# Routed experts in four groups of slots, each read back behind its own blocks, and a conditional tail of blocks

## The chip, the cores and the metric

The kernel runs on one core of one Trainium2 chip. The metric is the device time of one launch in microseconds (us): the median of several runs. A profiled execution is used to see where the time goes; it is slower than the unprofiled runs, and its own time is given beside theirs.

## The reference

The input is `x`, two sequences of 1024 tokens with 256 features. Two layers are applied, each of which runs its mixture-of-experts feed-forward before and after its attention part (feed-forward, attention, feed-forward, with halved feed-forward residuals). In the first layer (L0) the attention part is RWKV (time mix, then channel mix), in the second (L1) a linear attention that sums over the tokens of a sequence.

The feed-forward part, cut to what matters:

```python
def moe(x):                      # x is normalized; L0: E=8, K=2, H=176; L1: E=32, K=6, H=96
    scores = softmax(x @ gate_w) # L1: sigmoid
    topk_w, topk_i = top_k(scores, K)          # L1: weights divided by their sum
    comb = zeros(T, E); comb[t, topk_i] = topk_w
    g = silu(einsum('td,edf->tef', x, wg)) * einsum('td,edf->tef', x, wu)
    routed = einsum('tef,efd,te->td', g, wd, comb)
    shared = silu(x @ sg) * (x @ su) @ sd      # hidden width 2*H
    return routed + shared

def l1_attention(X):
    Q, K, V = split(X @ W_in.T + b_in); Q, K = rope(Q), rope(K)
    A = sum_over_tokens(K / norm(K) * V)       # one row per sequence
    return (A * Q) @ W_out.T + b_out + X
```

Each token goes to K experts only, so the routed part needs K, and not E, products per token.

## The kernel before

**Tiles.** The 2048 tokens are 16 tiles of 128 (`NT`), kept in SBUF as `x`. Four tiles (`BT`) are the unit in which normalization, transposes and router logits are made (`prep`), and eight tiles (`HT`) are a half; a half is also one sequence.

**Dispatch.** `sparse_moe` handles one feed-forward part. After two `prep`s `plan(h)` gives each pair (token, expert) of its half a slot: each expert's pairs are ranked by matmuls with a triangular matrix, each expert's region is rounded up to whole blocks of 128 slots, and the slot numbers go into `idx`. `scatter(h)` then writes the normalized rows to their slots in `xs`, a buffer in HBM, by one indirect DMA for each tile and each of its K choices (line 401, on POOL). L0 has 16 of these per half, L1 has 48. The second half fills up the open last block of each expert from the first half and then goes on in new blocks. Slots that hold no token read zeros, which `fill_slots` (line 260) writes once ahead. `owners` works out, for each block, the expert that owns it; `weights(h)` takes the routing weights of each pair into `wk`.

**Blocks.** A block is 128 slots of one expert. `blocks` is a software pipeline: `fetch` reads the block from `xs` (SP's queue, line 511), `features` transposes it (PE, line 520), `inner` makes gate and up with the expert's weights, which are chosen by a register (line 542), `turn` transposes the hidden values, and `outward` makes the down product (line 559), copies it from PSUM on DVE (`yb`, line 567) and stores it to `ys` in HBM. The number of blocks is the worst case: 39 for L0 and 127 for L1.

**Reading back.** `gather(t, k)` (line 578, on POOL) reads the result rows of a tile's k-th choices by an indirect DMA, and `add_back` (line 589, on DVE) adds them, weighted, to `x`. The first half's rows lie in the first 23 (L0) or 79 (L1) blocks at most, so its gathers may start when these are stored, beside the later blocks; the second half's gathers wait for all blocks (`first` and `NBLK` in `gather`). POOL's queue is worked in order, so scatters and gathers stand in one line.

**Shared part.** `shared(h)` makes the shared expert for eight tiles on PE, beside the scatters.

**Order of the whole.** L0's first feed-forward part; the fill of L1's slots and RWKV beside it; L0's second part with the weights of L1 loading; L1's first part; attention on the first sequence beside the last gathers, then the dispatch of its half, then attention on the second sequence and the dispatch of that half; L1's second part, whose last gathers end the kernel. Within that order the instructions of each engine are put in sequence by a scheduler when the program is built; the tile pools, with their fixed numbers of buffers by tag, add waits where a buffer is used again. In attention the normalized tiles `xl` and their transposes take buffers of the tags `xn` and `xT`, the same that hold `m2`'s normalized rows. PSUM has the tags `pa`, `pb`, `pt` and `py`, two banks each: blocks use all four, `prep` and `plan` use `pt`.

Of the kernel before, what the change touches and what calls it, by code (L numbers as in the profile page):

```python
# [39 lines left out]
def moe_blocks(m):  # L40
    return (NTOK * m["K"] + m["E"] * (P - 1)) // P
# [3 lines left out]
def macaron_kernel(ctx: ExitStack, tc: tile.TileContext, a: dict, out: bass.AP):  # L45
# [28 lines left out]
    row_i = const.tile([P, 1], I32, name="row_i")  # L74
    nc.gpsimd.iota(row_i, pattern=[[0, 1]], base=0, channel_multiplier=1)
    row = const.tile([P, 1], F32, name="row")
    nc.vector.tensor_copy(row, row_i)
# [6 lines left out]
    nc.gpsimd.memset(every, 1.0)  # L84

# [18 lines left out]
    def normalize(src, dst, n, name):  # L104

        mv = small.tile([P, n, 2], F32, tag="mv", name=f"mv_{name}")
        for i in range(n):
            st = small.tile([P, 6], F32, tag="st", name=f"st_{name}_{i}", bufs=4)
            nc.vector.bn_stats(st, src[i])
            nc.vector.bn_aggr(mv[:, i, :], st)  # L110
        rstd = small.tile([P, n], F32, tag="rstd", name=f"rstd_{name}")
        nc.scalar.activation(rstd, mv[:, :, 1], AF.Sqrt, bias=eps)
        nc.vector.reciprocal(rstd, rstd)
        for i in range(n):
            nc.vector.tensor_scalar(  # L115
                dst[i], src[i], mv[:, i, 0:1], rstd[:, i : i + 1], ALU.subtract, ALU.mult
            )
# [15 lines left out]
    def route(w, lg, name, taken=None, comb=None):  # L133
# [41 lines left out]
        else:  # L175
            tot = small.tile([P, BT], F32, tag="tot", name=f"tot_{name}")
            nc.vector.tensor_reduce(tot, comb, AX.X, ALU.add)
            nc.vector.tensor_scalar(tot, tot, 1e-20, None, ALU.add)
            nc.vector.reciprocal(tot, tot)
            nc.vector.tensor_scalar(tot, tot, 0.5, None, ALU.mult)  # L180
# [6 lines left out]
    def sparse_tiles(pool, layer):  # L187
# [17 lines left out]
            blocks=moe_blocks(m),  # L205
# [61 lines left out]
    HT = NT // 2  # L267
    WHO = 4

    def sparse_moe(layer, w, nth, xs, ys, moe, last=False):  # L270

        name = f"{layer}_{nth}"
        E, K, H, C, HP, NBLK = (w[k] for k in ("E", "K", "H", "C", "HP", "blocks"))
        SH, SU, rows = w["SH"], w["SU"], w["rows"]

        first = (HT * P * K + E * (P - 1)) // P
        xs, ys = xs[0 : NBLK * P, :], ys[0 : NBLK * P, :]
        taken = moe.tile([P, NT, E], F32, tag="taken", name=f"taken_{name}")
        comb = moe.tile([P, NT, E], F32, tag="comb", name=f"comb_{name}")
        past = moe.tile([P, NT + 1, E], F32, tag="past", name=f"past_{name}")  # L280
        slot = moe.tile([P, NT, E], F32, tag="slot", name=f"slot_{name}")
        top = back.tile([P, NT, 8], F32, tag="top", name=f"top_{name}", bufs=2)
        idx = back.tile([P, NT, K], I32, tag="idx", name=f"idx_{name}", bufs=2)
        wk = back.tile([P, NT, K], F32, tag="wk", name=f"wk_{name}", bufs=2)
        who = moe.tile([P, P], I32, tag="who", name=f"who_{name}", bufs=2)
        ends = moe.tile([P, 2, E], F32, tag="ends", name=f"ends_{name}")
        xn = [moe.tile([P, HT, D], F32, tag="xn", name=f"xn_{name}_{h}", bufs=2) for h in range(2)]
        xT = [
            moe.tile([P, DC, HT * P], F32, tag="xT", name=f"xTs_{name}_{h}", bufs=2)
            for h in range(2)  # L290
        ]
        scattered, stored, far = [], [], {}

        def prep(b):
            sub = f"{name}_{b}"
            h, o = divmod(BT * b, HT)
            ts = slice(BT * b, BT * b + BT)
            xb = [xn[h][:, o + i, :] for i in range(BT)]
            normalize(x[ts], xb, BT, sub)
            for c in range(DC):  # L300
                nc.scalar.copy(xT[h][:, c, o * P : o * P + TB], transposed(xb, c, sub))
            lg = bank("pt", f"lg_{sub}")[:, 0 : BT * E].rearrange("p (t e) -> p t e", e=E)
            for i in range(BT):
                for c in range(DC):
                    nc.tensor.matmul(  # L305
                        lg[:, i, :],
                        xT[h][:, c, (o + i) * P : (o + i + 1) * P],
                        w["router"][:, c, :],
                        start=(c == 0),
                        stop=(c == DC - 1),  # L310
                    )
            route(w, lg, sub, taken[:, ts, :], comb[:, ts, :])

        def running(src, sub):

            end, d = src, 1
            while d < E:
                nxt = small.tile([P, E], F32, tag="end", name=f"end_{sub}_{d}", bufs=3)
                nc.vector.tensor_copy(nxt[:, 0:d], end[:, 0:d])
                nc.vector.tensor_tensor(  # L320
                    nxt[:, d:E], end[:, d:E], end[:, 0 : E - d], ALU.add
                )
                end, d = nxt, 2 * d
            return end

        def plan(h):

            sub = f"{name}_{h}"
            ts = slice(HT * h, HT * h + HT)

            if h == 0:
                nc.vector.memset(past[:, 0, :], 0.0)
            for t in range(HT * h, HT * h + HT):
                nc.vector.tensor_tensor(
                    past[:, t + 1, :], past[:, t, :], taken[:, t, :], ALU.add
                )
            pr = bank("pt", f"rank_{sub}")[:, 0 : HT * E]
            nc.tensor.matmul(
                pr, before, taken[:, ts, :].rearrange("p t e -> p (t e)"), start=True, stop=False
            )  # L340
            nc.tensor.matmul(
                pr, every, past[:, ts, :].rearrange("p t e -> p (t e)"), start=False, stop=True
            )
            pn = bank("pt", f"count_{sub}")[:, 0:E]
            nc.tensor.matmul(pn, every, past[:, HT * h + HT, :], start=True, stop=True)

            over = moe.tile([P, E, NT], F32, tag="over", name=f"over_{sub}")
            nc.vector.tensor_tensor(
                over,
                pn.unsqueeze(2).to_broadcast([P, E, NT]),  # L350
                steps128.unsqueeze(1).to_broadcast([P, E, NT]),
                ALU.is_gt,
            )
            own = small.tile([P, E], F32, tag="own", name=f"own_{sub}", bufs=3)
            nc.vector.tensor_reduce(own, over, AX.X, ALU.add)
            if h == 1:
                nc.vector.tensor_tensor(own, own, far["own"], ALU.subtract)
            end = running(own, sub)
            if h == 0:
                nc.vector.tensor_copy(ends[:, 0, :], end)  # L360
            else:
                nc.vector.tensor_tensor(
                    ends[:, 1, :], end, ends[:, 0, E - 1 : E].to_broadcast([P, E]), ALU.add
                )
            base = small.tile([P, E], F32, tag="base", name=f"base_{sub}", bufs=3)
            nc.vector.tensor_tensor(base, ends[:, h, :], own, ALU.subtract)
            nc.vector.tensor_scalar(base, base, float(P), 1.0, ALU.mult, ALU.add)


            rank = pr.rearrange("p (t e) -> p t e", e=E)  # L370
            sl = slot[:, ts, :]

            def wide(v):
                return v.unsqueeze(1).to_broadcast([P, HT, E])

            if h == 0:
                nc.vector.tensor_tensor(sl, rank, wide(base), ALU.add)
                limit = small.tile([P, E], F32, tag="limit", name=f"limit_{sub}")
                nc.vector.tensor_scalar(limit, own, float(P), None, ALU.mult)
                far.update(own=own, base=base, limit=limit)  # L380
            else:


# [705 lines left out]
```

## Time and profile before

| | |
|---|---|
| time, median of 3 runs | 1545.19 us (1539.85 to 1549.84) |
| profiled execution, its own time | 1739.74 us |
| span in the profile | 1737.5 us |
| mean granted TensorE clock | 0.817 |
| busy: PE, DVE, ACT, POOL | 1202.7, 758.1, 578.8, 523.5 us |
| L0's first blocks, RWKV, L0's second blocks | about 130 to 245, 265 to 475, 575 to 715 us |
| L1's first blocks, L1's second blocks | about 925 to 1142, 1450 to 1665 us |
| gathers, scatters | 256 of 975 ns, 256 of 966 ns |

PE is TensorE's matmul, PEld its weight loads, DVE VectorE, ACT ScalarE, POOL GpSimd and SP SyncE. A line of a group of instructions has the source line, engine, operation and operands, the count, then after the bar the busy time in us and the mean duration of one in ns, then the idle time of the engine just before these instructions and what ended most of it. A line of the waits has who waited, for whom, the total in us, how often, and the longest.

### The profile page before, as it was taken

To read this page: it belongs to the slowest core of one execution; us is meant where nothing else is said; L and a number is where in the kernel's file an instruction comes from. 1 tells how busy PE (TensorE), PEld (TensorE's weight loads), DVE (VectorE), ACT (ScalarE), POOL (GpSimd) and SP (SyncE) were. 2 spreads that over 40 slices of the span, in tenths; PEclk is the share of its full clock that TensorE was granted. 3 is DMA by queue.
4 is the path that set the end of the run, shared out by engine and by line. 5 is a ranking of instruction groups with operands and counts; after the bars stand their busy time and mean duration, and the time that the engine had idled before them with its cause. 6 is when DMAs were issued, how large, how long until landed. Compare 5 with 4: busy or idle time off the path is not lost.

```text
span 1737.5 us, 20794 instructions
## 1 busy us (share of the span) xinstructions
PE 1202.7 (69%) x5462; PEld 907.0 (52%) x5462; DVE 758.1 (44%) x2588; ACT 578.8 (33%) x1552; POOL 523.5 (30%) x559
## 2 busy tenths in 40 slices
PE   6589867899976997510629996874734726997730
PEld 4467643566664775410418995742522515996630
DVE  5322349665243234412604444657705712444543
ACT  2123335776331333400105662421302203663310
POOL 1500222111124003175460006446171072004546
PEclk8699978899967998855759998986866767998975
DMA  9502327400082033542124665632030024666743
GB/s 273 179 27 92 119 85 254 157 1 1 1 186 82 25 104 118 134 142 78 52 103 123 188 186 176 205 92 85 22 106 18 8 104 140 185 188 183 210 133 107
DMA packets 182907, 203.01 MB, mean 117 GB/s; under 512 B 40044, under 2 KB 165772, under 8 KB 182796
## 3 DMA queue, kind: packets, MB, share of 16 engines
q1 hardware_dynamic: 158220, 134.55, 25.8%
q0 software_dynamic: 24576, 67.14, 12.3%
q8 instruction: 50, 0.82, 0.2%
q14 instruction: 61, 0.50, 0.1%
HBM read 100.68 MB, written 100.93 MB: 116 GB/s over the span
## 4 chain that ended last, share of the span: by engine, by line
PE 56%; DVE 11%; another core or an unknown queue 11%; issue 10%; DMA 5%; POOL 3%; ACT 2%; SPq 2%; POOLq 0%; DVEq 0%; ACTq 0%
PE pg_L_b L542 15%; PE py_L_b L559 10%; PE pg_L L454 5%; PE px_L L520 4%; PE py_L L496 4%; PE pkk_cm L705 3%; PE pkv_cm L717 3%; PE ph_L_b L470 3%; DMA yk_L<-ys_L,idx_L 3%; POOL xs_L L401 2%; DVE x L589 2%; PE lg_L L305 1%; PE ph_L L470 1%; DMA ys_L<-yb_L 1%
## 5 line engine op out<-in xcount | busy, mean ns | idle before, releaser
L578 POOL DMA_INDIRECT yk_L<-ys_L,idx_L x256 | 249.6, 975 | 715.1 <-DMA ys_L<-yb_L 418.2
L401 POOL DMA_INDIRECT xs_L<-xn_L,idx_L x256 | 247.4, 966 | 281.5 <-DVE idx_L L394 152.3
L445 DVE TENSOR_TENSOR h_L_b<-g_L_b,pg_L_b 128x96 f32<-128x96 f32 (+1 forms) x332 | 90.1, 271 | 334.5 <-ACT g_L_b L444 290.7
L542 PE MATMUL pg_L_b<-L1gu,xbT_L 128*128 x1016 | 215.9, 337 | 4.9 <-issue 3.4
L520 PE MATMUL px_L<-ident,xb_L 128*128 128x128 f32 x664 | 132.1, 282 | 79.8 <-DMA xb_L<-xs_L 46.6
L542 PEld LDWEIGHTS pg_L_b<-L1gu,xbT_L 128*128 128x128 f32 x1016 | 165.8, 197 | 24.0 <-issue 5.4
L589 DVE SCALAR_TENSOR_TENSOR x<-yk_L,wk_L,x 128x256 f32<-128x256 f32 x256 | 121.7, 478 | 96.9 <-DMA yk_L<-ys_L,idx_L 81.3
L559 PE MATMUL py_L_b<-L1down,hT_L_b 96*128 x508 | 157.1, 392 | 9.3 <-ACT hT_L_b L477 7.1
L567 DVE COPY yb_L<-py_L_b 128x256 f32<-128x256 f32 x332 | 140.0, 422 | 52.3 <-PE py_L_b L559 18.3
L444 ACT ACTIVATE g_L_b<-pg_L_b 128x96 f32<-128x96 f32 (+1 forms) x332 | 88.5, 266 | 206.2 <-PE pg_L_b L542 146.2
L520 PEld LDWEIGHTS px_L<-ident,xb_L 128*128 128x128 f32 x664 | 93.4, 145 | 110.4 <-DMA xb_L<-xs_L 47.0
L524 ACT COPY xbT_L<-px_L 128x256 f32<-128x256 f32 x332 | 123.0, 371 | 63.7 <-issue 51.1
L477 ACT COPY hT_L_b<-ph_L_b 96x128 f32<-96x128 f32 (+1 forms) x332 | 95.3, 287 | 130.2 <-PE ph_L_b L470 55.8
L123 PE MATMUL pt_L<-ident,xn_L 128*128 128x128 f32 x128 | 26.2, 350 | 121.1 <-DVE xn_L L115 103.4
L542 PE MATMUL pg_L_b<-L0gu,xbT_L 128*128 x312 | 107.7, 468 | 0.0
L470 PE MATMUL ph_L_b<-ident,h_L_b 128*96 128x128 f32 (+1 forms) x410 | 101.6, 279 | 3.6 <-issue 3.1
L454 PE MATMUL pg_L<-L0sgu,xTs_L 128*128 128x352 f32 x256 | 93.4, 501 | 2.0 <-DVE h_L L445 2.0
L559 PE MATMUL py_L_b<-L0down,hT_L_b 88*128 x312 | 83.1, 389 | 13.5 <-issue 8.2
L559 PEld LDWEIGHTS py_L_b<-L1down,hT_L_b 96*128 96x128 f32 x508 | 83.1, 197 | 11.9 <-ACT hT_L_b L477 8.6
L123 PEld LDWEIGHTS pt_L<-ident,xn_L 128*128 128x128 f32 x128 | 19.3, 182 | 127.3 <-issue 120.1
L445 DVE TENSOR_TENSOR h_L<-g_L,pg_L 128x176 f32<-128x176 f32 (+1 forms) x96 | 31.9, 340 | 122.5 <-ACT g_L L444 74.3
L559 PEld LDWEIGHTS py_L_b<-L0down,hT_L_b 88*128 88x128 f32 x312 | 60.4, 196 | 35.0 <-issue 9.7
(216 smaller groups left out, 1849.5 us busy)
## 6 DMA issues: line engine op xcount, KB each, us to landing
xb_L<-xs_L SPq DMA_DIRECT2D x332, 128.0 KB
ys_L<-yb_L SPq DMA_DIRECT2D x332, 128.0 KB
xs_L<-zero SPq DMA_DIRECT2D x1, 16256.0 KB
xs_L<-zero SPq DMA_DIRECT2D x1, 4992.0 KB
xs_L<-xn_L,idx_L POOLq DMA_INDIRECT x256
yk_L<-ys_L,idx_L POOLq DMA_INDIRECT x256
L1gu<-in_L_gate SPq DMA_DIRECT2D x8, 384.0 KB
L1gu<-in_L_up SPq DMA_DIRECT2D x8, 384.0 KB
```

What stands on the lines that cost most here:

```text
L401: d = nc.gpsimd.indirect_dma_start(out=xs, out_offset=bass.IndirectOffsetOnAxis(ap=idx[:, t, k : k + 1], axis=0), in_=xn[h][:, i, :], in_o ...
L445: nc.vector.tensor_tensor(dst, g, pg[:, width : 2 * width], ALU.mult)
L454: nc.tensor.matmul(pg, xT[half][:, c, i * P : (i + 1) * P], w["sgu"][:, c, u, :, :].rearrange("p z w -> p (z w)"), start=(c == 0), stop=(c ...
L470: nc.tensor.transpose(pt[0:m, k * P : (k + 1) * P], h[:, r : r + m], ident)
L477: nc.scalar.copy(hT[0:m, lo:hi, :].rearrange("p k t -> p (k t)"), pt[0:m, lo * P : hi * P])
L520: nc.tensor.transpose(px[:, c * P : (c + 1) * P], xb[:, c * P : (c + 1) * P], ident)
L524: nc.scalar.copy(xbT.rearrange("p c t -> p (c t)"), px[:, 0 : DC * P])
L542: nc.tensor.matmul(pg, xbT[:, c, :], w["gu"][:, c, bass.ds(e, 1), :, :].rearrange("p e z h -> p (e z h)"), start=(c == 0), stop=(c == DC - 1),
L559: nc.tensor.matmul(py, hT[0:HP, k, :], w["down"][:, bass.ds(e, 1), k, :].rearrange("p e d -> p (e d)"), start=(k == 0), stop=(k == C - 1),)
L567: nc.vector.tensor_copy(yb, py)
L578: d = nc.gpsimd.indirect_dma_start(out=yk, out_offset=None, in_=ys[0 : n * P, :], in_offset=bass.IndirectOffsetOnAxis(ap=idx[:, t, k : k + ...
L589: added = nc.vector.scalar_tensor_tensor(x[t], gathered.pop((t, k)), wk[:, t, k : k + 1], x[t], ALU.mult, ALU.add)
```

## The change

- **Four groups.** Slots are given out in four groups of four tiles (`plan(g)`, `scatter(g)`, `combine(g)`), where it was two halves. The rows of group g lie in the first 15, 23, 31, 39 blocks (L0) or 55, 79, 103, 127 blocks (L1), and its gathers wait for these alone. `plan` works with experts on partitions and small matmuls in place of a running sum on DVE; `owners` is rewritten for four groups.
- **The last blocks are conditional.** `owners` also yields the number of used blocks (`used`). For L1 the first 116 blocks are run always, and the last 11 only if `used` is over 116, by a branch. `ys` beyond block 116 is cleared ahead.
- **Writes between reads.** The dispatch of L1's first part runs between the blocks of L0's second part: after a group is read back, its four tiles are normalized, routed and planned, and each group's scatter is put behind the gathers of the next group. In L1's second part the scatter of a group comes right behind its own plan.
- **Buffers.** L1 has two slot buffers, `xs_L1_0` and `xs_L1_1`, each cleared at RWKV's start; attention hands its `xn` and `xT` tiles over to the dispatch (`given`). `xb` has five buffers.
- **Attention and norms.** Half of the normalized tiles are made on ACT. Attention takes its norms for eight tiles at once, sums over tokens by matmuls, adds the residual in fewer operations, and reads its sines and cosines from a compact table (`load_turns`).

The core of the diff:

```diff
+SURE = {"L0": moe_blocks(MOE["L0"]), "L1": 116}
...
+        first = [moe_blocks(w, BT * (g + 1)) for g in range(NB)]
...
-        def plan(h):
+        def plan(g):
...
+            pc = bank("pt", f"count_{sub}")
+            for t in range(lo, hi):
+                nc.tensor.matmul(
+                    pc[0:E, 0:1], taken[:, t, :], ones, start=(t == lo), stop=(t == hi - 1)
+                )
...
+            pr = bank("py", f"rank_{sub}")[:, 0 : BT * E].rearrange("p (t e) -> p t e", e=E)
+            nc.tensor.matmul(pr, before, taken[:, lo:hi, :], start=True, stop=False)
...
+            pb = bank("pt", f"far_{sub}")
...
-            n = first if t < HT else NBLK
+            n = first[t // BT]
...
-        def combine(h, lag=4):
+        def combine(g, lag=4):
...
+        def blocks():
+
+            g = 0
+            for n, _ in enumerate(some(0, sure)):
+                if g < NB and n == first[g] + 3:
+                    yield g
+                    g += 1
+            if sure < NBLK:
+                n = nc.values_load(
+                    used,
+                    engines=ENGINES,
...
+                with tc.If(n > sure):
+                    for _ in some(sure, NBLK):
+                        pass
+                yield g
...
-        fill_slots(xs["L1"], moe_blocks(MOE["L1"]), behind=m["latest"]["add"])
+        for k in range(2):
+            fill_slots(xs[f"L1_{k}"], moe_blocks(MOE["L1"]), behind=m["latest"]["add"])
+        fill_slots(
+            ys["L1"][SURE["L1"] * P :, :],
+            moe_blocks(MOE["L1"]) - SURE["L1"],
+            behind=m["latest"]["add"],
+        )
...
-    beside(m0["blocks"](2), ready, rate=0.5, after=36)
+    m1 = None
+    for g in m0["blocks"]():
+        m0["combine"](g)
+        if m1 is None:
+            m1 = sparse_moe("L1", w1, "L1_0", xs["L1_0"], ys["L1"], moe_pool)
+        if g > 0:
+
+            with tc.issue_after(m0["latest"]["row"]):
+                m1["scatter"](g - 1)
+        m1["prep"](g)
+        m1["plan"](g)
+    m1["scatter"](NB - 1)
...
+    def onward(g, out_of):
+        for t in range(BT * (g % 2), BT * (g % 2) + BT):
+            out_of(t)
+        m2["prep"](g)
+        m2["plan"](g)
+
+    for g in m1["blocks"]():
+        m1["combine"](g)
+    out_of = attention(0)
+    m2 = sparse_moe("L1", w1, "L1_1", xs["L1_1"], ys["L1"], moe_pool, given, last=True)
+    for g in (0, 1):
+        onward(g, out_of)
+
+        with tc.issue_after(m1["latest"]["row"]):
+            m2["scatter"](g)
+    out_of = attention(1)
+    for g in (2, 3):
+        onward(g, out_of)
+        m2["scatter"](g)
+    m2["owners"]()
...
+    for g in m2["blocks"]():
+        m2["combine"](g)
```

## The prediction

> **What bounds the kernel now.** I read the busy shares and slices first, then busy time by stage, then the waits, and last the timeline of POOL. The page:
>
> ```profile
> PE 1202.7 (69%) x5462; PEld 907.0 (52%) x5462; DVE 758.1 (44%) x2588; ACT 578.8 (33%) x1552; POOL 523.5 (30%) x559
> ...
> PE   6589867899976997510629996874734726997730
> ...
> POOL 1500222111124003175460006446171072004546
> ...
> L578 POOL DMA_INDIRECT yk_L<-ys_L,idx_L x256 | 249.6, 975 | 715.1 <-DMA ys_L<-yb_L 418.2
> L401 POOL DMA_INDIRECT xs_L<-xn_L,idx_L x256 | 247.4, 966 | 281.5 <-DVE idx_L L394 152.3
> ```
>
> No engine bounds all of it. The slices show PE full in some stretches and nearly empty in others, and POOL busy where PE is empty. POOL's time is 512 indirect transfers of about 0.97 us. The stages, as stretches:
>
> ```profile
> 575.00:715.00 140.00, 129.84 (x616) 97.97 (x615) 50.57 (x161) 54.96 (x155) 15.16 (x16) 0.96 0.27 83
> 715.00:850.00 135.00, 27.57 (x103) 21.26 (x104) 46.81 (x219) 14.12 (x23) 64.94 (x67) 0.54 0.38 109
> 850.00:925.00 75.00, 37.35 (x122) 23.21 (x121) 12.62 (x34) 7.74 (x23) 43.30 (x45) 0.66 0.25 88
> 925.00:1142.00 217.00, 194.93 (x1158) 170.12 (x1157) 112.68 (x345) 113.33 (x389) 47.58 (x48) 0.94 0.60 180
> 1142.00:1215.00 73.00, 41.58 (x111) 22.59 (x110) 46.16 (x140) 10.71 (x35) 48.08 (x48) 0.75 0.31 90
> 1215.00:1300.00 85.00, 49.17 (x178) 32.65 (x177) 34.27 (x161) 18.66 (x35) 38.62 (x41) 0.74 0.17 61
> 1300.00:1360.00 60.00, 34.59 (x118) 22.77 (x118) 34.80 (x115) 12.63 (x39) 7.52 (x8) 0.71 0.06 20
> 1360.00:1450.00 90.00, 28.66 (x121) 20.32 (x121) 30.78 (x140) 11.10 (x24) 46.50 (x48) 0.63 0.21 72
> 1450.00:1665.00 215.00, 192.93 (x1140) 168.60 (x1141) 100.46 (x300) 106.66 (x380) 46.61 (x48) 0.95 0.62 187
> 1665.00:1737.50 72.50, 1.10 (x4) 0.46 (x4) 24.37 (x51) 0.26 (x1) 45.33 (x48) 0.53 0.38 109
> ```
>
> The columns are the stretch, then busy us of PE, PEld, DVE, ACT and POOL with counts, the granted clock, the DMA share and GB/s. Rows 1, 4 and 9 are blocks: PE is over 89% busy, and a block costs 217/127 = 1.71 us (L1) or about 115/39 = 2.95 us (L0, from the first layer, 130 to 245 us). The other rows are transitions between layers, 590 us together, in which PE is busy 220 us. The waits name the hand-overs:
>
> ```profile
> POOL yk_L L578 <- DMA ys_L<-yb_L: 418.2, 5, 137.4
> ...
> POOL xs_L L401 <- DVE idx_L L394: 152.3, 4, 75.8
> ...
> DVE qk_at L854 <- remote: 41.7, 1, 41.7
> ```
>
> POOL stands idle until a half's last block is stored, or until a plan's addresses are out, and then runs 48 transfers at a fixed pace with PE waiting behind it. The third is DVE in attention on the second batch (1275 to 1316 us): its tiles take the buffers that the scatter of the second L1 layer still reads. The pace is seen in POOL's tail:
>
> ```profile
> 1669.46 0.94 POOL L578 DMA_INDIRECT yk_L<-ys_L,idx_L  x1 [20.60 <-DMA ys_L<-yb_L]
> 1670.71 0.94 POOL L578 DMA_INDIRECT yk_L<-ys_L,idx_L  x1 [0.30 <-issue]
> ```
>
> One gather each 1.25 us; scatters come each 1.27 us. So 48 are 60 us, 24 are 30 us.
>
> **What the Trainium skill says.** "DMA: Bandwidth & Descriptors", section "Anatomy of one DMA — SWDGE (gpsimd) path", gives such a DMA a fixed cost of about 2 us, mostly the receipt of the write. The trace agrees: a row of 128 KB lands 2.5 to 3 us after issue. "Perfetto Trace Analysis", section "DMA Instruction — SWDGE (GPSIMD)", says that the shown window ends with the descriptors, not the data; hence I price a queue by its pitch, and add the landing once at its end. The same page, section "Optimization Strategy", advises to interleave regimes with different limits; here that holds for transfers beside blocks, where row 4 takes 48 gathers without PE falling under 89%. "Advanced Engine Details and Errata", section "Control Flow Timing", prices a compare-and-branch at 108 ns. No branch is in this trace.
>
> **The change part by part.** The sum is made on the profiled execution (1739.74 us, span 1737.5); the median of the runs is 1545.19, so a saved us there is worth 1545.19/1739.74 = 0.888 in the forecast.
>
> *Conditional blocks.* Routing the reference's own inputs through the slot rule gives 114 used blocks in the first L1 layer and 112 in the second. Both are under 116, so 11 blocks are skipped twice: 2 x 11 x 1.70 = 37. In place come a drain of the block pipeline (which the end of the loop had anyway), a register load on four engines and a branch. The page "DMA: Bandwidth & Descriptors" (section "Latency and other measured facts") puts the floor of such a load at 0.6 us, which no row here shows. With the last store waited for on SP, I take 3 per layer (0.7 to 8). Net 31.
>
> *The last readback.* Before, 48 gathers follow the last block: 72.5 us. Built, the order has 21 of group 2's 24 gathers ahead of the branch, and 3 + 24 = 27 after it. Group 2 may start at block 103's store, 13 x 1.7 = 22 us before the end, while 21 gathers take 26. So: 4 over, 27 x 1.25 = 34, and 5 to land, add and write out = 43. Gain 29. The fewer blocks make less cover; without any it would be 48 gathers again and the gain nothing.
>
> *L0's second layer into L1's first* (575 to about 925, 350 us). Now each group of four tiles is read back, normalized, routed and planned between blocks. In the built order DVE does block 14's copy, then all adds, norms and the plan of group 0, and only then block 15's copy; likewise behind 22 and 30. POOL takes 8 gathers, 8, scatter of group 0 (24), 8, 24, 8, 48. Each stop is: store landing 2.5, 8 gathers 10, landing 2.5, then norm, transposes, logits, routing and plan. For the latter I take 21, from the same steps on eight tiles (41 us from attention's last tile at 1344 to its addresses at 1385, the output product in them). That is 36, and queued behind it are DVE's block copies, whose two "py" buffers then stop PE. Of the scatters, 30 us lie beside 8 blocks (24) and a stop, so they hide. So 118 (39 blocks and filling) + 3 x 36 + 2 + 10 + plan 21 + last 48 scatters 61 less the plan of group 3 that lies beside the first 24 (about 20), + 5 = 305. Gain 45. If two blocks in flight cover part of a stop (20 each) it is 93; at 50 each it is nothing. The shared product (16 tiles, some 50 us of PE) lies beside the last 61 us, as before.
>
> *L1's first layer into its second* (1142 to 1451, 309 us). From the last block T: branch +3; 27 gathers, 34 us. Built, DVE interleaves their adds with the first attention, which ends at about T+48. Group 0's output, norm and plan +31 (T+79), group 1 +21 (T+100), second attention +36 (T+136), since the scatter's tiles are handed to it instead of taken from it, and the 41.7 us wait goes. Then +31 (T+167) and +21 (T+188). Scatters of 24 follow each plan; the last two run T+167 to T+229. PE's 12 remaining shared tiles at 4.6 us end at T+243. Blocks start at about T+240. Gain 69 (40 to 90): what is late next is the DVE chain of four plans, and PE's shared product just behind the scatters.
>
> *Slots cleared.* Two L1 buffers and 1.4 MB are filled beside RWKV. One fill took 49 us at 348 GB/s (275 to 324), and three share one zero tile, so POOL's second clearing of it waits for the first fill and POOL's adds of RWKV stand behind it. The first such add in before is at 321, the next set at 375, when the second fill would be done (324 + 49): cost 3 (0 to 15).
>
> *Small edits.* L0's first layer ends with 8 gathers instead of 16: 10 less, but three group starts at about 2 each: +5. Half of the norms go to ACT (33% busy); attention has fewer DVE operations; four plans for two, 16 small matmuls for DVE sums, table loads: -5 (+-10).
>
> Sum: 31 + 29 + 45 + 69 - 3 + 5 - 5 = 171. 1739.7 - 171 = 1568.7; x 0.888 = 1393.
>
> **The rivals.** (B) The stops between L0's blocks are mostly covered: 20 each, and the L1 transition is at its better end: 171 + 48 + 15 = 234, time 1337. For it: DVE is 36% busy in row 1. Against it: the built order puts all of a plan ahead of the next copy. (C) The transitions stay as long as before, since one plan more per half and the same number of transfers eat what overlap brings: 31 + 29 and only the 41.7 us wait, less a few: about 95, time 1461. For it: PE and POOL take turns in the transitions because data depend on each other. Against it: in rows 5 to 8 PE is busy a third to under 60% and POOL 13 to 66%, so neither is full. (D) Slower: the stops in the L0 loop grow, as DVE holds block copies behind a plan, and POOL holds a group's 8 gathers behind 24 scatters. It turns the sign when each of three stops costs 36 + 171/3 = 93; at 100 it is 1739.7 + 21, or 1564. That needs another 60 us per stop, twice the 30 us of a whole scatter, so it is unlikely. (E) A count is over 116, and the branch is taken in both: 1393 + 0.888 x 37 = 1426, with the tail's gain smaller.
>
> **How the numbers follow.** A 0.50, B 0.17, C 0.22, D 0.05, E and its like 0.06. The forecast is A's. The range 1335 to 1470 takes in B and C, the bounds of the L0 stage (0 to 93) and of the L1 transition (40 to 90); it leaves out D and the ends. About 1% is what a measurement tells from no change: faster by more 0.92 (A, B, E and nearly all of C), same 0.03 (the worst end of C), slower 0.05 (D).
>
> **What would show it.** Right: 116 stores of blocks per L1 layer instead of 127, a tail of about 43 us after the last block with 27 gathers; three gaps of about 36 us in PE between L0's second blocks; no 41.7 us wait at attention; L1's two block stages about 240 us apart. Wrong: PE gaps over 60 us in the L0 loop, a hole of more than 10 us at the branches, POOL's adds in RWKV late by tens of us, or a transition of 300 us between the L1 layers.

## The result: 0.995 of the kernel before

The changed kernel takes 1536.55 us (median of 20 runs, 1533.72 to 1542.96), the kernel before 1544.82 us (20 runs); the ratio is 0.9947 with a 95% interval of 0.9935 to 0.9959. So it is faster by half a per cent, 8 us, where 1393 us and some 150 us of gain were forecast. One fact is needed to read every number below: on some chips (three of the five in the runs below) all runs of the kernel before take about 1545 us, on others all take 1727 to 1750 us, and the profile that the prediction was summed on (1739.74 us) looks like the second level; runs are set against each other at one level only. The profile after, 1537.43 us with a span of 1535.6, is of the first, which is called the usual level below; the other is called the slower one.

The page of the changed kernel, the lines that answer to those shown of before:

```profile
PE 1231.9 (80%) x5752; PEld 946.7 (62%) x5752; DVE 724.0 (47%) x2444; ACT 598.2 (39%) x1541; POOL 527.9 (34%) x561
...
PE   6699995699998799577546899887679887998850
...
POOL 2420132011112500116647300565627374006655
...
L668 POOL DMA_INDIRECT yk_L<-ys_L,idx_L x256 | 248.8, 972 | 601.5 <-DMA ys_L<-yb_L 481.2
L463 POOL DMA_INDIRECT xs_L<-xn_L,idx_L x160 | 155.8, 974 | 124.3 <-issue 43.3
```

The last two rows are the gathers and most of the scatters (96 more read attention's tiles): still 512 transfers of 0.97 us. The stages of the changed kernel, columns as before: L0's second blocks; from there to L1's blocks; L1's blocks; the transition; L1's second blocks; the tail:

```profile
594.00:796.00 202.00, 138.97 (x593) 105.96 (x591) 71.96 (x263) 55.58 (x137) 72.02 (x75) 0.75 0.35 105
796.00:878.00 82.00, 55.19 (x250) 42.11 (x251) 33.07 (x124) 18.24 (x47) 52.30 (x54) 0.72 0.43 138
878.00:1064.00 186.00, 169.88 (x1022) 147.73 (x1020) 105.78 (x324) 101.41 (x348) 60.65 (x63) 0.99 0.67 201
1064.00:1300.00 236.00, 180.08 (x723) 132.79 (x722) 130.62 (x477) 60.93 (x143) 131.01 (x130) 0.73 0.24 79
1300.00:1487.00 187.00, 168.59 (x1014) 148.79 (x1012) 96.77 (x289) 94.02 (x338) 61.89 (x64) 0.97 0.68 206
1487.00:1535.60 48.60, 0.00 (x0) 0.00 (x0) 17.49 (x37) 0.00 (x0) 30.76 (x33) 0.50 0.41 117
```

In the first row PE is busy 69% of the time, not 93% as in the blocks of before: these are the stops for the plans. The last row is the shortened tail. The waits:

```profile
POOL yk_L L668 <- DMA ys_L<-yb_L: 481.2, 10, 94.1
...
DVE x L680 <- DMA yk_L<-ys_L,idx_L: 146.6, 148, 6.8
...
POOL xs_L L463 <- DVE idx_L L455: 94.7, 5, 32.3
```

POOL still waits for stored blocks and for addresses, only in more and shorter pieces. The second line will matter: VectorE's adds wait 146.6 us for their rows (139.4 us in the kernel before at the usual level, so the waits as such are not new).

### The profile page after: what moved, and what is told of

Read it like the earlier page. It is cut to its first block, busy times and chain, and to the rows that moved or that the text cites. A ratio compares the mean times of both kernels' runs of the same rounds, so it can differ in the third digit from the quotient of the medians.

```text
span 1535.6 us, 21133 instructions
## 1 busy us (share of the span) xinstructions
PE 1231.9 (80%) x5752; PEld 946.7 (62%) x5752; DVE 724.0 (47%) x2444; ACT 598.2 (39%) x1541; POOL 527.9 (34%) x561
## 5 line engine op out<-in xcount | busy, mean ns | idle before, releaser
L463 POOL DMA_INDIRECT xs_L<-xn_L,idx_L x160 | 155.8, 974 | 124.3 <-issue 43.3
L632 PE MATMUL pg_L_b<-L1gu,xbT_L 128*128 x928 | 194.2, 333 | 1.6 <-PE ph_L_b L561 0.9
L680 DVE SCALAR_TENSOR_TENSOR x<-yk_L,wk_L,x 128x256 f32<-128x256 f32 x256 | 122.7, 482 | 148.8 <-DMA yk_L<-ys_L,idx_L 146.6
L632 PEld LDWEIGHTS pg_L_b<-L1gu,xbT_L 128*128 128x128 f32 x928 | 148.4, 193 | 14.9 <-PE ph_L_b L561 1.9
L657 DVE COPY yb_L<-py_L_b 128x256 f32<-128x256 f32 x310 | 130.3, 421 | 55.1 <-PE py_L_b L649 34.0
L649 PE MATMUL py_L_b<-L1down,hT_L_b 96*128 x464 | 142.2, 389 | 3.8 <-DVE yb_L L657 2.8
L610 PE MATMUL px_L<-ident,xb_L 128*128 128x128 f32 x620 | 121.6, 278 | 18.9 <-DMA xb_L<-xs_L 15.7
L463 POOL DMA_INDIRECT xs_L<-axl_at,idx_L x96 | 96.4, 1004 | 82.4 <-DVE idx_L L455 53.8
L614 ACT COPY xbT_L<-px_L 128x256 f32<-128x256 f32 x310 | 114.5, 370 | 22.3 <-PE px_L L610 18.9
L632 PE MATMUL pg_L_b<-L0gu,xbT_L 128*128 x312 | 110.1, 478 | 0.3
L649 PEld LDWEIGHTS py_L_b<-L1down,hT_L_b 96*128 96x128 f32 x464 | 76.2, 194 | 7.1 <-ACTq L726 1.8
L561 PEld LDWEIGHTS ph_L_b<-ident,h_L_b 128*96 128x96 f32 (+1 forms) x388 | 48.2, 127 | 44.0 <-DVE h_L_b L536 35.9
```

The lines of the kernel that those rows point to most:

```text
L463: d = nc.gpsimd.indirect_dma_start(out=xs, out_offset=bass.IndirectOffsetOnAxis(ap=idx[:, t, k : k + 1], axis=0), in_=xb[:, i, :], in_offs ...
L561: nc.tensor.transpose(pt[0:m, k * P : (k + 1) * P], h[:, r : r + m], ident)
L610: nc.tensor.transpose(px[:, c * P : (c + 1) * P], xb[:, c * P : (c + 1) * P], ident)
L614: nc.scalar.copy(xbT.rearrange("p c t -> p (c t)"), px[:, 0 : DC * P])
L632: nc.tensor.matmul(pg, xbT[:, c, :], w["gu"][:, c, bass.ds(e, 1), :, :].rearrange("p e z h -> p (e z h)"), start=(c == 0), stop=(c == DC - 1),
L649: nc.tensor.matmul(py, hT[0:HP, k, :], w["down"][:, bass.ds(e, 1), k, :].rearrange("p e d -> p (e d)"), start=(k == 0), stop=(k == C - 1),)
```

## The experiments

**The kernel before, profiled once more.**

> The kernel before, unchanged, profiled once more. Theory 1, the profiled execution that the prediction was summed on (1739.7 us) was not a usual one and its extra 195 us lie in stages and not in a common factor: this execution takes 1540 to 1550 us with a span of about 1543, the first 600 us stand as before (L0's second blocks begin at about 605 us), and some 190 us are gone from the transitions after 715 us (215, 309 and 72 us there). Theory 2, a profile stretches this kernel as a whole: about 1740 us again, and every stage as before. Theory 3, the extra is a lower clock of TensorE: the transitions stay, and the two stretches of L1's blocks (217 and 215 us) are shorter.

Measured: 1547.0 us, ratio 1.0006 (0.9995 to 1.0018), span 1543.8. Its stages, cut as above:

```profile
562.00:676.00 114.00, 103.49 (x504) 77.89 (x502) 52.02 (x196) 49.15 (x127) 15.38 (x16) 0.97 0.41 115
676.00:833.00 157.00, 56.75 (x235) 43.72 (x236) 51.98 (x202) 21.84 (x53) 108.73 (x112) 0.62 0.39 125
833.00:1028.00 195.00, 184.36 (x1123) 160.96 (x1122) 111.22 (x340) 111.13 (x378) 48.03 (x48) 0.99 0.66 197
1028.00:1283.00 255.00, 146.58 (x555) 97.37 (x554) 147.88 (x557) 56.46 (x144) 141.19 (x144) 0.75 0.25 80
1283.00:1474.00 191.00, 181.13 (x1112) 160.31 (x1110) 100.73 (x299) 104.74 (x370) 47.20 (x48) 0.99 0.69 208
1474.00:1543.80 69.80, 0.00 (x0) 0.00 (x0) 23.22 (x48) 0.00 (x0) 45.39 (x48) 0.51 0.38 107
```

Here is the base that the forecast lacked. Behind L0's second blocks POOL is busy 109 of 157 us with 112 transfers in one line; between the L1 layers it is busy 141 of 255 us with 144. The first theory holds in kind. Counted from block copy to block copy (`yb`) in both profiles, the transitions are shorter by 44 us (168 for 212, L0 to L1) and by 61 us (256 for 316, between the L1 layers). It misses that the first 600 us are shorter too, by 43 us, L0's second blocks by 10, and the L1 blocks by 16 and 18, these in the part beside gathers. The line "DVE qk_at L854 <- remote: 41.7" has no counterpart: in that attention VectorE never waits over 6 us here. And profiling does not slow the kernel: this profiled execution took 1546.06 us, like the unprofiled runs beside it. The chain that ended last, first in the profile before:

```profile
PE 56%; DVE 11%; another core or an unknown queue 11%; issue 10%; DMA 5%; POOL 3%; ACT 2%; SPq 2%; POOLq 0%; DVEq 0%; ACTq 0%
```

and in the same kernel profiled again:

```profile
PE 52%; DMA 16%; POOL 11%; DVE 10%; issue 8%; ACT 3%; SPq 1%; POOLq 0%; DVEq 0%; ACTq 0%
```

"Another core or an unknown queue" was 11% of 1737.5, 191 us, in a program on one core, and the second chain has no such entry. That the two spans differ by 194 us is no proof that this is the same time: other profiles of the slower level have 4% or nothing of it in their chains. What tells the levels apart is the list of waits. All eight profiles that took the longer time have waits that end with "remote", a releaser that the profile cannot name, 187 to 392 us of idle time in sum over the engines (294 in the profile before); none of the twelve profiles at the usual level has one.

With this, the times between the first and last copies of blocks divide the 8 us:

| stretch, us | before, again | changed | difference | forecast |
|---|---|---|---|---|
| start to L0's first block | 129.7 | 140.7 | +11 | about 0 |
| to L0's second blocks | 432.5 | 453.5 | +21 | about 0 |
| to L1's blocks | 270.6 | 284.2 | +14 | -45 |
| L1's blocks | 194.6 | 184.5 | -10 | -16 |
| to L1's second blocks | 255.7 | 237.5 | -18 | -69 |
| L1's second blocks | 190.0 | 186.0 | -4 | -16 |
| tail | 70.7 | 49.2 | -21 | -29 |

**All blocks, no branch.**

```diff
-SURE = {"L0": moe_blocks(MOE["L0"]), "L1": 116}
+SURE = {"L0": moe_blocks(MOE["L0"]), "L1": moe_blocks(MOE["L1"])}
```

> The changed kernel with all 127 blocks of L1 run unconditionally, and so no branch, no count read and no clearing of the result's tail. If the skipped blocks bring what their own duration is worth, 2 x 11 x 1.60 us (116 blocks from 878 to 1063 us in the changed kernel's trace) less about 3 us for each branch: 25 to 35 us slower than the changed kernel, so 1.010 to 1.025 of the kernel before or so. If the tail's shorter cover matters more (the last group's gathers then start behind 127 blocks but with the third group's done), less: 10 to 20 us slower.

The clearing of `ys` beyond block 116 is left out with it. Measured: 1555.34 us, 1.0058 (1.0038 to 1.0077) of before, 19 us over the changed kernel. The second reading holds: L1's blocks take 203 and 204 us instead of 184.5 and 186, so 11 blocks are worth 18 us in each layer, but the transition behind the first is 6 us shorter and the tail behind the second 41 us instead of 49, since the third group's gathers have more cover. L0's first and second blocks start within 1 us of the changed kernel's, so no cost of the clearing is seen there. The branch itself costs little: behind the first L1 layer PE goes on 0.5 us after its last block, and attention's first product then waits 4.8 us for VectorE to be past the branch.

**The dispatch behind the blocks.**

```diff
     for g in m0["blocks"]():
         m0["combine"](g)
-        ...
-        m1["prep"](g)
-        m1["plan"](g)
+    for g in range(NB):
+        m1["prep"](g)
+        m1["plan"](g)
+        m1["scatter"](g)
```

> The changed kernel with one part undone: L1's first dispatch (norms, plans, scatters) stands behind all of L0's second blocks and their readback, in four groups, instead of between the blocks. In the changed kernel the stretch from L0's second first block to L1's first block is 284 us (594 to 878), in the kernel before, profiled again, 271 (562 to 833). Theory 1, the three stops of 31 us in the block loop cost as much as they hide: 115 us of blocks, 12 for the last 8 gathers, 122 for 96 scatters in one line and 12 to the first block, 261 us, so about 20 us faster than the changed kernel (1515). Theory 2, placing the writes between the reads is a gain, and the loss against before lies elsewhere: about 10 to 40 us slower (1545 to 1575), since 48 scatters of 61 us come out into the open.

Measured: 1511.21 us, 0.9768 (0.9742 to 0.9795), 25 us under the changed kernel. From L0's second first block to L1's first it is 254 us (595 to 849) instead of 284. So placing the writes between the reads, as built, is a loss: L0's blocks take 188 us from first to last copy for 103 here, and from there to L1's first block it is 96 us for 151. Three stops of 31 us cost 85 us and hide 55 us of the 61 that 48 scatters take.

**L0 in two groups.** The same, with the size of a group made a parameter of `plan`, `scatter`, `combine` and `first`: eight tiles in L0, four in L1.

> As the kernel with the dispatch behind the blocks, and L0's slots in two groups of eight tiles instead of four of four, in both of its parts; L1 keeps four groups. Against the kernel before, profiled again, the changed kernel reaches L0's first blocks 11 us later (141 against 130) and from the end of RWKV's readers to L0's second blocks it takes some 20 us longer. Theory 1, that is the price of four plans in a row instead of two: 20 to 30 us faster than four groups with the dispatch behind the blocks, in all some 1490. Theory 2, it comes from other edits (half of the norms on ScalarE, the weights ahead of the shared product, the fills): within 5 us of the four groups.

Measured: 1491.38 us, 0.9624 (0.959 to 0.9658), 20 us less again. L0's first block is at 130.1 us as in the kernel before, its second blocks at 570.6. L0's first block was at 143.6 and its second blocks at 594.7 with four. So four plans in a row, as built, were the price; the norms on ScalarE and the order of `weights` are the same in both.

**A PSUM bank of the routing's own.** Blocks, shared product and plans share the tag "pt", whose two buffers are handed out in the order of the program.

```diff
     def bank(tag, name):
-        return psum.tile([P, TB], F32, tag=tag, name=name)
+        bufs = 1 if tag in ("pt", "pp") else None
+        return psum.tile([P, TB], F32, tag=tag, name=name, bufs=bufs)
...
-            lg = bank("pt", f"lg_{sub}")...
+            lg = bank("pp", f"lg_{sub}")...
-            pr = bank("py", f"rank_{sub}")...
+            pr = pz[:, 0 : BT * E]...     # pz = bank("pp", ...): count, rank and far in one bank
...
```

The edit takes the routing out of "pt" and, with the ranks, out of "py" at once; which of the two made the stops is not told apart.

> The changed kernel, dispatch between blocks as it was, but the routing's transposes, logits, plan and owners use a PSUM bank with a tag of its own, one buffer, and the tag of the blocks' second transposes has one buffer instead of two. Theory 1, the stops of 31 us between L0's second blocks come from PSUM buffers handed out in program order, which put VectorE's work of a whole plan ahead of the next block's copy: the stops go, L1's first block comes 40 to 70 us earlier, less what one buffer costs the 310 blocks (0 to 0.1 us each): 1475 to 1510. Theory 2, the stops come from the chain itself, readback to norm to plan on an engine that works in order: the stops stay near 30 us and the time within 10 us of the changed kernel, or over it by the blocks' single buffer.

Measured: 1496.01 us, 0.967 (0.9639 to 0.97). The stops of 31 us are gone, with the dispatch still between the blocks; L1's first block comes at 814 us. It comes early in L0's first part too (133.5 for 140.7). But L1's blocks grew to 197 and 194 us from 184.5 and 186, which put the one buffer of "pt" under suspicion. So the spare buffer was taken elsewhere (in RWKV, every other product of the tag "pb" goes into the new bank too):

```diff
-        bufs = 1 if tag in ("pt", "pp") else None
+        bufs = 1 if tag in ("pb", "pp") else None
```

> The routing's own PSUM bank taken from pb, once more with the changed kernel beside it. On a chip where the kernel before takes 1545: about 1478 if the one buffer of the second transposes cost the blocks their time, 1490 to 1505 if any single buffer does. In any state, against the changed kernel of this call: 0.96 to 0.975 by the first theory.

Measured: 1465.67 us, 0.9493 (0.944 to 0.9546), with the changed kernel at 1537.32 us (0.995, 0.9931 to 0.9968) on the same chip:

> The changed kernel, unchanged, beside its three variants on one chip. In the last call the kernel before took 1735 us in every run instead of 1545, so its ratios cannot be set against the earlier ones without the changed kernel beside them. If the kernel before takes 1545 here: 1536. If it takes 1735 here, two theories: the extra time is a share of all stages, and the ratio stays 0.995 (1726); or it is paid in the stages between blocks, once for each stop of the block loop too (its stops between L0's blocks were 52 us instead of 31 in the kernel with the later adds), and the ratio lies near 0.985 to 1.0 with the stops longer.

The gain is 72 us, 12 more than forecast: the ratio to the changed kernel is 0.953, below the forecast 0.96 to 0.975. In the traces of these two, 47 us of it lie between L0's second first block and L1's, 14 ahead of L0's first blocks, 9 between the L1 layers and 5 ahead of L0's second blocks. So the stops are two thirds of it. The rest lies where dispatches run beside other work; L0's first block comes at 128 us with four plans in a row, so it was the shared buffers that made these dear. One stop of the changed kernel (31 us, from a copy to the next one), from its profile:

```profile
681.00:712.00 31.00, 14.34 (x64) 11.68 (x62) 10.33 (x46) 6.47 (x12) 21.12 (x23) 0.62 0.34 110
```

and L0's second blocks, the way to L1's blocks and these blocks with the bank:

```profile
576.00:706.00 130.00, 118.13 (x573) 86.08 (x572) 61.75 (x223) 53.17 (x137) 53.27 (x55) 0.96 0.47 138
706.00:809.00 103.00, 55.67 (x269) 40.37 (x268) 38.05 (x163) 24.76 (x50) 71.43 (x74) 0.70 0.43 142
809.00:998.00 189.00, 173.62 (x1027) 150.32 (x1026) 104.26 (x325) 101.78 (x351) 59.95 (x63) 0.97 0.66 198
```

From the first to the last copy of these blocks it is 126 us instead of 188, with the same work between them and PE busy 91%. About 20 of these 62 us are matmuls that ran faster: PE was busy 139 us with 593 of them at a granted clock of 0.75 where the stops were, and 118 us with 573 at 0.96 without. L1's blocks (188 and 185 us) are hardly slower for the single "pb" (185 and 186 in the changed kernel beside it), so it was the single "pt" that stretched them. "Perfetto Trace Analysis" in the Trainium skill, section "Optimization Strategy", says that a gap that repeats can mean too little SBUF or PSUM for the next tile; here three gaps of 31 us went when the routing got a bank of its own.

The same edit was measured on the slower level, and in the kernel before:

> As the changed kernel with a PSUM bank of its own for the routing (1496), but the bank is taken from the tag pb, which blocks use for their first transposes and the shared product for every other gate, and the blocks' second transposes keep two buffers. There, L1's blocks took 1.70 and 1.67 us each on the mean against 1.60 and 1.62 in the changed kernel. Theory 1, the one buffer of the second transposes did that: 116 x (0.10 + 0.05), some 18 us come back and the time is about 1478, since the first transposes only wait for one copy of 0.37 us. Theory 2, any tag cut to one buffer costs the blocks as much: 1490 to 1505.

> The kernel before with the same PSUM edit as the fastest variants: the routing gets a bank of its own, taken from pb, and nothing else changes. Theory 1, the bank's worth is that it lets a dispatch run between blocks, of which the kernel before has little: within 12 us of the kernel before. Theory 2, it is worth as much to any dispatch, beside the shared product as well: 25 to 70 us faster (1475 to 1520).

At that level the changed kernel takes 0.984 (0.9793 to 0.9886, two runs) of the kernel before; with the bank, on another chip, 0.9575 (0.9536 to 0.9614); the kernel before with the bank takes 0.9871 (0.9838 to 0.9904), 23 us less. Over the 0.984, 0.9575 is 2.7% less, against 1.3% in the kernel before. The 23 us lie between the two theories: the bank helps a dispatch that does not run between blocks as well, but less. At the usual level the kernel before was not run with it.

**Copies on ScalarE.** From the first group's readback on, every second `yb` copy of L1 by `nc.scalar.copy`.

> The changed kernel, with every second block's copy out of PSUM in L1, from the first group's readback on, made by ScalarE instead of VectorE. A block of L1 takes 1.42 us without gathers beside it and 1.7 to 2.1 with them. Theory 1, VectorE is the bound there: 0.27 + 0.42 + 1.36 adds of 0.48 us is 1.34 us a block and the adds wait in line; half of the copies gone is 0.21 us a block over about 60 blocks in each of two layers: 15 to 25 us faster (1512 to 1522). Theory 2, the transfers slow each other (a block's fetch beside a gather) or the adds' waits do it: within 5 us of the changed kernel.

Measured: 1538.76 us, 0.9943 (0.9919 to 0.9966): nothing. Taking copies off VectorE does not help, so its amount of work is not the bound beside the gathers. The waits of the changed kernel from 965 to 1000 us say what it does:

```profile
DVE x L680 <- DMA yk_L<-ys_L,idx_L: 9.6, 10, 1.8
...
DVE h_L_b L536 <- ACT g_L_b L535: 1.7, 3, 0.7
```

An add stands in VectorE's order and waits for its row; the next block's work behind it should then wait too, which the next run tries.

**The adds later.** In L1's first two groups an add follows its gather seven rows behind and is queued behind a block's copy:

```diff
+                    with tc.issue_after(latest["copy"]):
+                        add_back(*pairs[n - lag])     # lag 7 for 4; 1.13 adds a block
...
```

> The later adds, once more with the changed kernel beside it. Against the changed kernel of this call 15 to 25 us less if the adds' waits ahead of the blocks' work are what slows blocks beside gathers (0.984 to 0.990), within 5 us if the transfers are.

Measured: 1520.89 us, 0.9845 (0.9821 to 0.987), 16 us less. The adds' waits in the whole run fall from 146.6 us to this:

```profile
DVE x L680 <- DMA yk_L<-ys_L,idx_L: 101.3, 105, 6.7
```

The first group's 24 gathers in L1's first layer, in the changed kernel and then here:

```profile
958.00:990.00 32.00, 27.09 (x165) 23.65 (x164) 20.07 (x63) 14.59 (x55) 23.41 (x24) 1.00 0.79 235
```

```profile
960.00:992.00 32.00, 32.00 (x206) 29.19 (x205) 23.75 (x72) 18.95 (x68) 23.06 (x24) 1.00 0.91 276
```

The same transfers at the same pace leave PE no idle time once the adds stand later, so there it was the place of the adds and not the transfers. Beside the first two groups' gathers a block takes 1.5 to 1.7 us instead of 1.8 to 2.0, and 1.42 us without gathers; what the remaining difference is stays open. L1's blocks come down to 170 and 172 us from 185 and 186; the transition and the tail give 9 us of that back. On the slower level:

> The changed kernel, where in L1 the adds of the first two groups' rows stand later in VectorE's order: seven rows behind the gather instead of four, one to 0.88 blocks, each behind a block's copy. In the changed kernel's trace from 965 to 1000 us VectorE's adds wait 9.6 us for their rows, ahead of the blocks' work. Theory 1, those waits and not the transfers are why a block takes 1.7 to 2.1 us beside gathers: two groups in two layers, 4 x about 24 blocks at 0.2 to 0.3 us less, 15 to 25 us faster (1512 to 1522). Theory 2, it is the transfers' bandwidth: within 5 us of the changed kernel.

it was 0.9761 (0.9703 to 0.9818), beside the 0.984 (0.9793 to 0.9886) of the changed kernel on another chip of that level; these intervals overlap, so the gain is shown at the usual level only.

**Both.**

> Both edits, once more with the changed kernel beside it: if they add, 0.945 to 0.96 of the changed kernel of this call, so 1460 where that takes 1536.

Measured: 1444.2 us, 0.9349 (0.9329 to 0.9369): 93 us under the changed kernel where the two apart gave 72 and 16, and 0.939 of it, a little below the forecast range. The gains add, so the two causes are apart. This is the fastest version, 6.5% under the kernel before. On the slower level:

> Both of the edits of this call to the changed kernel: the routing's own PSUM bank taken from pb, and the later adds. If the two causes are apart, their gains add: with 1478 and 1517 as their middles, about 1460. If they share a cause, not under the better of the two.

it was 0.9489 (0.945 to 0.9529); the order of the variants is the same.

**L1 in two groups as well**, otherwise as the kernel with L0 in two groups.

> L0 and L1 in two groups of eight tiles, the dispatch behind the blocks, on whatever level this chip has. Where the kernel before takes 1545: 1515 to 1530 if reading back four groups in L1 is a gain (1491 with L1 in four groups and L0 in two), 1483 to 1499 if gathers beside blocks cost as much as they save. Where it takes 1735 to 1746: 1680 to 1700 as in the two runs there.

Measured: 1498.08 us, 0.9664 (0.9625 to 0.9704), against 0.9624 (0.959 to 0.9658) with L1 in four, on another chip of the usual level. The intervals overlap: reading back four groups is not shown to bring anything. In the traces the tail is 72 us instead of 50, but L1's blocks take 175.5 and 175 us instead of 186 and 184, and the transition is 241 in both. In the kernel before, whose readback is in two groups too, these blocks take 194.6 and 190 us, so skipping 11 of them shows as 19 and 15 us here. On the slower level the same kernel came to 0.969 and 0.9687, with the changed kernel at 0.984:

> The kernel with L0 in two groups and the dispatch behind the blocks (1491), with L1 in two groups of eight tiles as well; the conditional blocks, the two slot buffers and the attention stay as changed. Theory 1, reading back four groups in L1 is a gain: 48 instead of 27 gathers follow the last block, 21 x 1.25 = 26 us more at the end and some 20 more between the L1 layers, less about 5 for each layer, whose blocks have fewer gathers beside them: 1520 to 1530. Theory 2, gathers beside blocks cost as much as they save: within 8 us of 1491.

> L0 and L1 in two groups of eight tiles, the dispatch behind the blocks, once more, since the chip of its first run had another level. If reading back four groups in L1 is a gain: 1515 to 1530, against 1491 with L1 in four groups. If gathers beside blocks cost as much as they save: 1483 to 1499.

**The change on the level of its forecast.**

> The changed kernel once more, as the measure for the others of this call, and in case that the kernel before takes 1735 us here: then about 1715 to 1735 (the ratio of 0.985 to 1.0, since the stops of its block loop grow too); 1537 where the kernel before takes 1545.

Measured: 1716.81 us (two runs), against 1746.02 for the kernel before. By stages (profile before, then this run): L0's second blocks to L1's 325 and 350 us, forecast 45 less; L1's blocks 211 and 218, forecast 16 less; transition 316 and 273, forecast 69 less; L1's second blocks 208 and 216, forecast 16 less; tail 71 and 46, forecast 29 less; the rest is equal within 2. So even against its own base the forecast of -171 was off by about 142.

## Why the prediction was wrong

The step that failed most is L0's second layer, which was to gain 45 us and lost 14 at the usual level, 25 at the slower level on which it was summed. Next is the base between the L1 layers. At the usual level the shortfalls against the sum of 171 are about 59 us from L0's second blocks to L1's, 51 between the L1 layers, 29 up to L0's second blocks, 17 in L1's blocks and 8 in the tail.

*L0's second layer, gain 45.* The stops were foreseen, with their place and nearly their size: 3 x 36 = 108 us forecast, and L0's blocks took 85 us more than in the kernel before (188 for 103), 113 at the slower level, where the second and third stop were 53 and 49 us. What failed is what they were to buy. First, the base of 350 us begins at 575, which is not yet a block:

```profile
575.00:594.00 19.00, 19.00 (x84) 14.00 (x84) 5.49 (x15) 5.18 (x19) 0.00 (x0) 1.00 0.01 2
```

PE makes the shared product here; the first block is fetched at 594.0 and its copy comes at 605.4. The 305 us start with the blocks, so some 20 us of the gain were never there. Second, the sum leaves 79 us from L0's last block to L1's blocks, where the runs show 96 us between the copies, 124 at the slower level, and 168 and 212 in the kernel before. So stops of 85 us bought 72. The cause of the stops, PSUM buffers that routing and blocks share, was named only for "py"; with a bank of the routing's own they are gone.

*The base and the factor 0.888.* The step "a saved us there is worth 0.888" took the profile's excess over the median as a stretch of everything. It was not: the same kernel at the usual level has 194 us less, of which 105 lie in the two transitions that the change was to shorten. Between the L1 layers the forecast for the changed kernel itself came true (240 us forecast, 237 measured), but the base was 256 and not 309, so the gain was 18 and not 69. That 305 and 284 lie near each other for L0 to L1 is luck: the 305 were summed on the slower level, and there it is 350. Nor is the level the whole error, since the changed kernel gained 29 us on that level, too, and not 171.

*The 41.7 us wait* was put down to attention's buffers. At the usual level the kernel before, with the same buffers, has no such wait. It belonged to the other level, as its releaser "remote" does.

*Skipped blocks, net 31.* The branch was sized right, and so was a block: 18 us for 11 of them in each layer with the branch undone, 19 and 15 us with L1 in two groups. What failed is that gathers beside blocks were costed at nothing, because "48 gathers" lay there "without PE falling under 89%". With four groups 62 and 63 gathers start beside L1's blocks, for 48 before, and the blocks take some 10 us longer in each layer than with two (186 and 184 for 175.5 and 175). So L1's two block stages fell by 10 and 4 us only. The later adds bring back 15 and 14 us, so most of that cost is the place of the adds.

*The last readback, gain 29.* Right in mechanism and nearly in size: 21. After the last copy 33 gathers start, not 27.

*Small edits, -5 (+-10) and +5.* The dispatch of four plans in L0 was the mis-sized term: +11 and +21. With L0 in two groups they are 0 and +8, with four plans and a bank of the routing's own -2 and +15; where the rest comes from is open.

*Clearing the slots, -3,* is not contradicted: from L0's last gather to the first scatter of its second part it is 239 us, and 236 before, at the usual level. POOL's second clearing of the zero tile did wait for the first fill (10.5 us, to 300.0). RWKV's first add on POOL, read as 321, is at 294.7 in the profile before.

Of the rivals, (C) was nearest in kind, the transitions' gain eaten, but its 1461 rested on the same base. Of (D)'s longer stops, the slower level shows 49 to 53 us, far from the 93 that it needed. The sign of the forecast was right, its size wrong by a factor of 18; and the sign is partly luck, since the stages that gained (53 us) barely outweigh those that lost (46 us). Not explained by a run is which part of attention's rewriting, the handing over of tiles and the two slot buffers brings how much: together with the skipped blocks they are about 50 us, what the kernel with two groups in both layers gains on before, of which 34 lie in L1's blocks by the traces.

## What to carry to other kernels

When the profiled execution is 13% longer than the median, as here, don't scale: find where the excess lies, by waits that name no instruction, or by a second profile, before a stage is used as a base. Let a base and its forecast begin at the same instruction. Work placed between the steps of a pipeline may need buffers of its own, in PSUM too; with shared tags it became a barrier here that cost more than it hid (85 us for 55). An operation that waits for a transfer, queued ahead of a pipeline's work on the same engine, held that work up here (16 us). A mean per block that mixes blocks with and without side work hides what the side work costs.

## What the runs showed of the hardware

The same kernel has two levels, 1545 and 1727 to 1750 us, each steady over all runs on one chip. On the slower one there are waits without a named releaser, most of them of ScalarE and VectorE (207 and 87 us in the profile before). The clearest case is the sigmoid of the routing on ScalarE, which often stands still while POOL issues scatters. A stop of the changed kernel there:

```profile
712.03 1.28 ACT L197 ACT_TABLE_LOAD   x1
...
734.30 0.96 POOL L463 DMA_INDIRECT xs_L<-xn_L,idx_L  x1 [0.30 <-issue]
736.71 0.28 ACT L197 ACTIVATE s_L<-lg_L 128x128 f32<-128x128 f32 x1 [23.39 <-issue]
```

and the same one at the usual level, where scatters run from 694 to 725 us as well:

```profile
701.06 1.28 ACT L197 ACT_TABLE_LOAD   x1
...
704.33 0.28 ACT L197 ACTIVATE s_L<-lg_L 128x128 f32<-128x128 f32 x1 [1.98 <-PE lg_L L351]
```

The logits were complete about 21 us before the sigmoid began on the slower level, and at once on the other. Four sigmoids of that run waited 15 to 23 us so, each with scatters in POOL's queue; a fifth, at 1361.8 us, began after 2 us although scatters ran from 1352.6 to 1382.7. So scatters alone do not do it. What holds the sigmoids, and whether the level belongs to the chip or to its condition, these runs don't tell.
